# A two-layer attention network on one core: layer 1's weight product at the start, biases as rows, and the order of VectorE's work in the FFN

## The chip, the cores and the metric

The kernel runs on one core of one Trainium2 chip. The metric is the device time of one execution in microseconds (us), as a median over several runs. One further execution was profiled; durations quoted from the trace belong to that one.

## What is computed

The input is x, 8 images of 32x32 pixels with 384 channels, so 1024 tokens of 384 channels an image. The reference, cut to what matters:

```python
x = x + L0(_gn(x))                       # layer 0, _gn: group norm, 32 groups
t = tokens(x)
t = t + L1_attn(_ln_t(t), Wq, Wk, Wv)    # layer 1, _ln_t: layer norm
t = t + L1_ffn(_ln_t(t))

# L0: 6 heads of 64
q, k, v = split(x @ qkv_w + qkv_b)
attn = (q * SCALE) @ k.T + rel_h + rel_w # rel_h, rel_w: q times relative position tables
out = softmax(attn) @ v
return out @ proj_w + proj_b

# L1_attn: one head of 384, causal
q, k, v = x @ Wq, x @ Wk, x @ Wv
return softmax(causal(q @ k.T * 384**-0.5)) @ v

# L1_ffn
h = gelu(bitlinear(x, W1, b1))
return bitlinear(h, W2, b2)

# bitlinear: W by the sign of W - mean, per group; then the result is scaled
# by its absolute maximum (per group of images) and clipped
y = x @ sign(W - mean(W)).T + b
return clip(y * QB / (max(abs(y)) + EPS), -QB + EPS, QB - EPS)
```

The FFN works in five groups of 8 // 5 = 1 image, so images 0 to 4 go through it; the others receive zeros from it.

## The kernel before

**Tiles and stages.** Images are taken in the order 5, 0, 1, 2, 3, 4, 6, 7. An image lies as channels on the 128 partitions: 3 slabs (NC = 3) of 128 channels by 1024 tokens, f_gnT in the profile. PSUM has one pool, ps_o, of eight buffers of one bank each (128x512 float32); every product of TensorE (PE) goes into the next of them that is free, by `o_tile`.

**Order.** The program is written as one stream, and a scheduler places the instructions on the engines and gives each tile a buffer. `behind_of(i)` and `tc.issue_after(i)` bind an instruction to stand behind instruction i in the order. Each engine then runs its instructions in order and waits by semaphores. DMAs are issued by SyncE (SP) and ScalarE (ACT), each in its own order.

**Start.** `run` calls `load_T` (three slabs of image 5, 512 KB each), then `load_weights`: the biases bqk, bv and b1 on ACT's queue, read element by element into one column for each 128 channels; the two relative position tables `rel`; and on SP's queue the three thirds of qkv_w (wq_sb, raw_1, raw_2; 576 KB each), wproj, proj_b as pb, wv and b2. `group_norm_T` makes statistics on VectorE (DVE) (L401, L402), averages over a group with two small products on PE (gmean L405, gvar L413), and normalises the slabs (L418). GpSimd (POOL) makes combinations of the weights for the products below (`weight_forms`).

**Layer 0.** Queries: f_qk (L508), 24 passes for the first, then the relative tables f_rel. Keys and values are made by 15 products (A to F, f_pr_A to f_pr_F) of combined weights with combined inputs; ACT and DVE combine their results (parts n0 to n6, m5 and so on: f_u_n, f_u_m) into f_k and f_v (L752). When the last copy of the values is made, ACT runs a one-column exponential `early` (L783), so that the table of the exponential is there. It reads the part n5, which DVE makes (L589).

`attend0_fast` goes over three pairs of heads and two halves of the queries. For each, `scores(p, c, half)` makes eight column tiles c: two score tiles, one for each head of the pair, with two matmuls each (f_s, L830 and L834), then one exponential each on ACT (L841) into f_pr. `add_up` sums on DVE (L846, L848), `values` multiplies by f_v (f_av, L856), and `reciprocals` gives the denominators.

**Joint bias and joint weights.** For the first image alone, `join_biases` multiplies the values' bias by wproj and adds proj_b (matmuls L357, addition L360 on DVE); it stands after the products of image 5. `multiply_out` loads the transposed Wq and Wk of layer 1 on SP's queue and multiplies them once to wqk (L371, 18 passes; scaled on DVE, L372), which later gives layer 1 queries against its inputs without keys. It stands after the first eight calls of `scores` of image 5.

**FFN.** For a token tile j of 128 tokens, `activate` makes the gelu twice on ACT (L1170): `hi`, rounded to a shorter format, and the exact value; DVE takes the residue `lo` (L1171). The second product y2 (L1188) multiplies hi and lo; DVE adds the bias (L1189) and takes the absolute maximum of the tile (L1190, am2). Tile 0 is cut in three parts, later tiles in two. In the program tile j's activations stand before its matmuls, and its bias addition before tile j + 1's activations.

Of the kernel before, what the change touches and what calls it, by code (L numbers as in the profile page):

```python
# [11 lines left out]
F32 = mybir.dt.float32  # L12
# [79 lines left out]
def conv_attn_hybrid(  # L92
# [37 lines left out]
    wqkv_sb = wf.rearrange("p r s o -> p (r s o)")[:, : NC * 3 * C].rearrange("p (k o) -> p k o", k=NC)  # L130
    bqk, bqk_neg, bv, b1_sb = (tile_of(n, [P, w]) for n, w in (("bqk", 6), ("bqk_neg", 6), ("bv", NC), ("b1_sb", NM)))
    pb, b2_sb = tile_of("pb", [P, C]), tile_of("b2_sb", [P, C])
# [4 lines left out]
    def load_weights(pools):  # L137

        nc.scalar.dma_start(out=bqk, in_=qkv_b[0 : 2 * C].rearrange("(m p) -> p m", p=P))
        nc.vector.memset(rel, 0.0)  # L140
        for half in range(2):
            nc.scalar.dma_start(out=rel[half * HD : (half + 1) * HD, 0, : 2 * H - 1], in_=rel_hT)
            nc.scalar.dma_start(out=rel[half * HD : (half + 1) * HD, 1, : 2 * W - 1], in_=rel_wT)
        nc.scalar.dma_start(out=bv, in_=qkv_b[2 * C : 3 * C].rearrange("(m p) -> p m", p=P))
        nc.scalar.dma_start(out=b1_sb, in_=b1.rearrange("(m p) -> p m", p=P))
        src = qkv_w.rearrange("(p k) o -> p k o", k=NC)
        raw = [wq_sb]
        for i in range(3):
            if i:
                raw.append(pools.flat(f"raw_{i}")[:, : NC * C].rearrange("p (k o) -> p k o", k=NC))  # L150
            nc.sync.dma_start(out=raw[i], in_=src[:, :, ts(i, C)])
        nc.sync.dma_start(out=wproj_sb, in_=proj_w.rearrange("(k p) o -> p k o", p=P))
        nc.sync.dma_start(out=pb, in_=proj_b.partition_broadcast(P))
        nc.sync.dma_start(out=wv_sb, in_=wv.rearrange("(k p) o -> p k o", p=P))
        nc.sync.dma_start(out=b2_sb, in_=b2.partition_broadcast(P))

        nc.scalar.mul(bqk[:, 0:NPAIR], bqk[:, 0:NPAIR], qscale)
        nc.scalar.mul(bqk_neg, bqk, -1.0)
        nc.scalar.mul(rel, rel, 1.0 / qscale)
        early = pools.small.tile([P, 1], F32, tag="early", name="early_root")  # L160
        nc.scalar.activation(early, ones[:, 0:1], AF.Sqrt)
        return raw
# [199 lines left out]

    def multiply_out(pools):
        both = pools.flat("wqkT")
        wqT_sb, wkT_sb = (both[:, i * NC * C : (i + 1) * NC * C].rearrange("p (k c) -> p k c", k=NC) for i in range(2))
        nc.sync.dma_start(out=wqT_sb, in_=wqT.rearrange("(k p) c -> p k c", p=P))
        nc.sync.dma_start(out=wkT_sb, in_=wkT.rearrange("(k p) c -> p k c", p=P))
        for m in range(NC):
            ps = pools.o_tile(f"wqk_{m}")
            for k in range(NC):  # L370
                nc.tensor.matmul(ps[:, :C], wqT_sb[:, k, ts(m, P)], wkT_sb[:, k, :], start=(k == 0), stop=(k == NC - 1))  # L371
            nc.vector.tensor_scalar_mul(wqk[:, m, :], ps[:, :C], C**-0.5)  # L372

    def stages(pools):

        last_transpose = [None]

# [16 lines left out]
        def group_norm_T(b, xT=None):  # L394
# [17 lines left out]
            ps = pools.o_tile(f"gvar_{b}")  # L412
            nc.tensor.matmul(ps[:, 0:1], over_group, d[:, 1:2], start=True, stop=True)  # L413
            nc.vector.tensor_scalar_add(d[:, 0:1], ps[:, 0:1], 1e-5)
# [207 lines left out]
        def layer0(b, xT):  # L622
# [133 lines left out]
            def products():  # L756
# [25 lines left out]
                with behind_of(of_v.last_copy):  # L782
                    exp_loaded[0] = nc.scalar.activation(early, of_v.part["n5"][:, 0:1], AF.Exp, scale=0.0).ins  # L783

# [16 lines left out]
            for p in () if pools.fast else range(1, NPAIR):  # L801
                later(p, None, None)
            if pools.fast and b == ORDER[0]:
                join_biases(pools)

            def residual():
# [7 lines left out]
        def attend0_fast(residual, b, q, k, r, v, later):  # L814
# [72 lines left out]
            for p, half in itertools.product(range(NPAIR), range(2)):  # L887
                t, last = ts(half, 512), (p, half) == (NPAIR - 1, 1)
                prs = [scores(p, c, half) for c in range(NJ)]
                if b == ORDER[0] and (p, half) == (0, 0):  # L890
                    multiply_out(pools)
                if b == ORDER[0] and (p, half) == (2, 0):
# [223 lines left out]
        def ffn(xt, b, gn):  # L1116
# [45 lines left out]

            last_gelu = [None]

            def activate(room, j, m0, m1):
                part = pairs[j // 2][:, m0:m1, j % 2, :]
                hi, lo = (room[:, i, m0:m1, :] for i in range(2))
                for dst in (hi, part):
                    with behind_of(last_gelu[0]):
                        last_gelu[0] = nc.scalar.activation(dst, part, AF.Gelu, scale=s).ins  # L1170
                nc.vector.scalar_tensor_tensor(lo, part, QB - QEPS, hi.bitcast(F32), ALU.min, ALU.subtract)  # L1171
                return [[(h[:, m - m0, :], w2m[m]) for m in range(m0, m1)] for h in (hi, lo)]

            y = pools.flat(f"y2_{b}")[:, : NJ * C].rearrange("p (j c) -> p j c", j=NJ)
            am2 = pools.small.tile([P, NJ], F32, tag="am2", name=f"am2_{b}")
            for j in range(NJ):
                ps = pools.o_tile(f"y2_{b}_{j}")
                room = pools.flat(f"hilo_{b}_{j}", F32R)[:, : 3 * T].rearrange("p (i m q) -> p i m q", i=2, q=P)
                if j == 0:
                    (hi0, lo0), (hi1, lo1), (hi2, lo2) = (activate(room, j, *cut) for cut in ((0, 3), (3, 6), (6, NM)))  # L1180
                    products = hi0 + hi1 + lo0 + lo1 + hi2 + lo2
                else:
                    products = [t for cut in ((0, 6), (6, NM)) for kind in activate(room, j, *cut) for t in kind]
                if j == 4:
                    xt = pools.flat(f"xagain_{b}")[:, : NJ * C].rearrange("p (j c) -> p j c", j=NJ)
                    nc.sync.dma_start(out=xt.rearrange("p j c -> p (j c)"), in_=spilt)
                for i, (h, w) in enumerate(products):
                    nc.tensor.matmul(ps[:, :C], h, w, start=(i == 0), stop=(i == len(products) - 1))  # L1188
                nc.vector.tensor_tensor(y[:, j, :], ps[:, :C], b2_sb, ALU.add)  # L1189
                nc.vector.tensor_reduce(am2[:, j : j + 1], y[:, j, :], AX.X, ALU.max, apply_absolute_value=True)  # L1190
# [27 lines left out]

        def run(pools):
            gn = load_T(ORDER[0])  # L1220
            if pools.fast:
                raw = load_weights(pools)
                plain.append(raw[0])
            else:
                load_plain()
                plain.append(wqkv_sb)
            for _ in group_norm_T(ORDER[0], gn):
                pass
            if pools.fast:
                xf[ORDER[0]] = image_forms(ORDER[0], gn, nc.vector)  # L1230
                with tc.issue_after(weight_forms(pools, nc.gpsimd, raw[1], 1)):
                    weight_forms(pools, nc.gpsimd, raw[2], 2)
                make_unit(pools)
                make_fold()
# [86 lines left out]
```

## Time and profile before

| what | value |
|---|---|
| median of 3 runs | 2328.33 us (2328.3 to 2329.42) |
| profiled execution, its own time | 2329.14 us |
| its span in the trace | 2326.9 us |
| PE busy | 2296.9 us (99%) |
| DVE, ACT, POOL busy | 1530.0 (66%), 1098.6 (47%), 416.0 (18%) |
| granted clock of PE, mean | 0.998 |
| DMA | 185.82 MB in 156242 packets, of which 113568 under 512 bytes; mean 80 GB/s |

The profile page gives each engine's busy time and its share of the span. The view of waits sums for each line of an engine how long it stood idle and what ended the wait: total, times, longest. The chain follows the work that ended last from the last instruction back to what released it. The timeline lists groups of instructions by start; the numbers are the start, the time that the group takes (until its last instruction ends), the engine, the line, the operation and its tiles. Names such as f_qk are the tiles' names in the program with the image left out; PEld is PE's loading of weights, POOL is GpSimd.

### The profile page before, as it was taken

The page shows a single profiled execution, that of the slowest core. Times are in us where ns is not written, and L with a number is a line of the kernel's source. Part 1 is how long each engine was busy: PE and PEld are TensorE (multiplying, and loading weights), DVE is VectorE, ACT ScalarE, POOL GpSimd, SP SyncE. Part 2 cuts the span into 40 slices and gives each one's busy share as a digit, 9 for nine tenths or more (in the row PEclk, how much of TensorE's full clock was granted, in tenths as well). Part 3 has the DMA queues.
Part 4 walks back from the last instruction along what each step waited for, and adds up shares of the span by engine and source line. Part 5 has one row for each costly group of instructions (what it writes and reads, how often), then busy time and mean ns, then how long its engine had stood idle before and what let it go on. Part 6 is the DMA issues. An engine that isn't in the chain of part 4 may idle for free.

```text
span 2326.9 us, 27722 instructions
## 1 busy us (share of the span) xinstructions
PE 2296.9 (99%) x9970; PEld 1318.8 (57%) x9970; DVE 1530.0 (66%) x2434; ACT 1098.6 (47%) x1874; POOL 416.0 (18%) x520
## 2 busy tenths in 40 slices
PE   7999999999999999999999999999999999999998
PEld 3545554558645577545685455774457754555454
DVE  6785578575887347884458864588834788527851
ACT  4551166137563257642376522757324666116611
POOL 4320322030140201310102302013020131021300
PEclk9999999999999999999999999999999999999999
DMA  6530471140630114520308202064002262017100
GB/s 158 157 92 26 135 155 37 55 163 28 145 100 28 42 67 109 130 62 1 109 28 179 67 27 95 22 156 109 28 27 82 80 156 64 1 48 161 37 1 29
DMA packets 156242, 185.82 MB, mean 80 GB/s; under 512 B 113568, under 2 KB 126208, under 8 KB 153280
## 3 DMA queue, kind: packets, MB, share of 16 engines
q1 hardware_dynamic: 135856, 114.66, 20.0%
q0 software_dynamic: 17184, 69.22, 9.5%
q8 instruction: 82, 1.34, 0.2%
q14 instruction: 64, 0.52, 0.1%
q10 hardware_dynamic: 3056, 0.08, 0.1%
HBM read 83.24 MB, written 50.33 MB: 57 GB/s over the span
## 4 chain that ended last, share of the span: by engine, by line
PE 97%; DVE 1%; ACT 1%; DMA 0%; issue 0%; POOL 0%; ACTq 0%
PE f_s L830 14%; PE f_av L856 14%; PE f_s L1018 8%; PE f_av L1033 8%; PE f_y L1143 7%; PE f_y L1188 7%; PE f_pj L455 5%; PE f_v L455 5%; PE f_q L977 5%; PE f_qk L508 5%; PE f_s L834 4%; PE f_pr_A L508 4%; PE f_pr_B L508 3%; PE f_rel L508 2%; PE f_pt L383 1%; PE f_pr_D L508 1%
## 5 line engine op out<-in xcount | busy, mean ns | idle before, releaser
L841 ACT ACTIVATE f_pr<-f_s 128x512 f32<-128x512 f32 x768 | 412.7, 595 | 40.4 <-PE f_s L834 35.2
L830 PE MATMUL f_s<-f_q,f_k 64*128 64x512 f32 x1536 | 401.5, 595 | 0.4 <-DVE f_v L752 0.2
L848 DVE TENSOR_TENSOR f_sum<-f_sum,f_pr 128x1024 f32<-128x1024 f32 x288 | 365.0, 1267 | 22.9 <-ACT f_pr L841 0.7
L856 PE MATMUL f_av<-f_pr,f_v 128*64 128x512 f32 x1536 | 339.3, 594 | 0.0
L834 PE MATMUL f_s<-f_r,unit 64*128 64x512 f32 x768 | 310.3, 791 | 0.0
L830 PEld LDWEIGHTS f_s<-f_q,f_k 64*128 64x128 f32 x1536 | 148.0, 186 | 125.9 <-issue 64.0
L856 PEld LDWEIGHTS f_av<-f_pr,f_v 128*64 128x64 f32 x1536 | 106.2, 137 | 196.3 <-issue 192.4
L1018 PE MATMUL f_s<-f_q,f_lnT 128*128 128x512 f32 (+3 forms) x576 | 195.9, 488 | 0.0
L1033 PE MATMUL f_av<-f_v,f_pr 128*128 128x385 f32 x576 | 195.3, 486 | 0.0
L1027 ACT ACTIVATE f_pr<-f_s 128x512 f32<-128x512 f32 (+3 forms) x96 | 46.9, 491 | 279.0 <-DVE f_s L1023 233.4
L726 POOL DMA_DIRECT2D f_r<-f_far x192 | 102.3, 535 | 403.9 <-DVE f_far L720 190.7
L1033 PEld LDWEIGHTS f_av<-f_v,f_pr 128*128 128x128 f32 x576 | 108.3, 190 | 77.2 <-issue 11.5
L1018 PEld LDWEIGHTS f_s<-f_q,f_lnT 128*128 128x128 f32 x576 | 102.0, 190 | 77.8 <-issue 53.8
L1154 DVE TENSOR_REDUCE am<-f_h 128x1 f32<-128x1024 f32 (+2 forms) x80 | 71.6, 946 | 95.8 <-ACT f_h L1147 95.8
L1188 PE MATMUL f_y<-f_w2a,f_hilo 128*128 128x384 f32 x640 | 128.9, 342 | 5.5 <-DVE f_hilo L1171 5.3
L1147 ACT ACTIVATE f_h<-f_y,b_sb 128x256 f32<-128x256 f32 x240 | 100.8, 472 | 67.0 <-PE f_y L1143 67.0
L508 PE MATMUL f_qk<-f_gnT,wq_sb 128*128 128x512 f32 x288 | 129.4, 601 | 1.5 <-DVE f_gnT L418 1.5
L977 PE MATMUL f_q<-f_lnT,wqk 128*128 128x512 f32 x288 | 127.5, 592 | 0.0
L455 PE MATMUL f_pj<-wproj_sb,f_oT 128*128 128x384 f32 x384 | 127.3, 488 | 0.0
L834 PEld LDWEIGHTS f_s<-f_r,unit 64*128 64x128 f32 x768 | 76.5, 187 | 89.5 <-issue 89.3
L455 PE MATMUL f_v<-wv_sb,f_lnT 128*128 128x384 f32 x384 | 126.5, 486 | 0.0
L519 POOL TENSOR_TENSOR f_xf<-f_gnT 128x512 f32<-128x512 f32 x28 | 35.5, 1277 | 503.0 <-DVE f_gnT L418 503.0
(215 smaller groups left out, 3517.6 us busy)
## 6 DMA issues: line engine op xcount, KB each, us to landing
f_far<-f_far SPq DMA_DIRECT2D x48, 512.0 KB, 5.0
f_r<-f_far SPq DMA_DIRECT2D x192, 128.0 KB, 2.9
f_r<-f_far POOLq DMA_DIRECT2D x192, 128.0 KB, 4.6
f_gnT<-in_xT SPq DMA_DIRECT2D x24, 512.0 KB, 4.6
f_far<-f_far SPq DMA_DIRECT2D x192, 64.0 KB, 4.7
f_x<-in_x SPq DMA_DIRECT2D x32, 384.0 KB, 7.9
f_w1a<-w1s POOLq DMA_DIRECT2D x5, 1536.0 KB, 6.9
f_w2a<-w2s POOLq DMA_DIRECT2D x5, 1536.0 KB, 9.1
```

Source lines behind the costliest of these rows:

```text
L455: nc.tensor.matmul(ps[:, :C], xT[:, k, ts(j, P)], w[:, k, cols], start=(k == 0), stop=(k == NC - 1))
L508: last_product[0] = nc.tensor.matmul(*args, **kw).ins
L830: nc.tensor.matmul(sc[par], k[rows[par], p, ts(c, P)], q[rows[par], p, ts(half, 512)], start=True, stop=False)
L834: last_matmul[0] = nc.tensor.matmul(sc[par], unit[rows[par], c // 2 % 2].rearrange("i h w -> i (h w)"), r(2 * (c // 4) + c % 2, p)[rows[pa ...
L841: last_exp[0] = nc.scalar.activation(pr[:, ts(par, 512)], sc[par], AF.Exp).ins
L848: adds.append(nc.vector.tensor_tensor(total, total, pr, ALU.add).ins)
L856: last_matmul[0] = nc.tensor.matmul(av[ts(par, HD), :], v[:, c, ts(2 * p + par, HD)], pr[:, ts(par, 512)], start=(c == 0), stop=(c == NJ - 1),
L977: nc.tensor.matmul(ps, wqk[:, k, ts(m, P)], xT[:, half, k, :], start=(k == 0), stop=(k == NC - 1))
L1018: nc.tensor.matmul(sc[:, lo:], xT[:, c // 4, k, ts(c % 4, P)], q[:, half, k, lo:], start=(k == 0), stop=(k == NC - 1),)
L1033: nc.tensor.matmul(av[:, : C + 1], prs[c][:, ts(j - c, P)], v[:, c, :], start=(c == 0), stop=(c == j))
L1143: nc.tensor.matmul(ps, w1k[i // 2][:, ts(m, P)], xs[i % 2][:, half, i // 2, :], start=(i == 0), stop=(i == 2 * NC - 1))
L1188: nc.tensor.matmul(ps[:, :C], h, w, start=(i == 0), stop=(i == len(products) - 1))
```

## The change

- `load_factors`, split off from `multiply_out`, is called first in `run`, ahead of the first image: wqT on SP's queue, wkT on ACT's. `multiply_out` follows right after `load_weights`.
- The biases are loaded as 21 rows of 128 elements (9 of qkv_b, 12 of b1), transposed by PE into one bank and copied by DVE into `biases`, of which bqk, bv and b1_sb are columns.
- wproj is loaded ahead of qkv_w. `join_biases` is called after the first group norm, bound behind the product gvar of it (`last_mean`).
- `early` reads the part n6, which ACT makes, in place of n5.
- In the FFN, tile j + 1's activations stand in the program ahead of tile j's bias addition, and that addition is bound behind the first residue (`first_lo`) of tile j + 1.

```diff
--- before.py
+++ after.py
@@ -128,7 +128,8 @@
     wproj_sb, wv_sb = (tile_of(n, [P, NC, C]) for n in ("wproj_sb", "wv_sb"))
     wf, wq_sb = tile_of("wf", [P, N_PROD, 2, P]), tile_of("wq_sb", [P, NC, C])
     wqkv_sb = wf.rearrange("p r s o -> p (r s o)")[:, : NC * 3 * C].rearrange("p (k o) -> p k o", k=NC)
-    bqk, bqk_neg, bv, b1_sb = (tile_of(n, [P, w]) for n, w in (("bqk", 6), ("bqk_neg", 6), ("bv", NC), ("b1_sb", NM)))
+    biases, bqk_neg = tile_of("biases", [P, 3 * NC + NM]), tile_of("bqk_neg", [P, 6])
+    bqk, bv, b1_sb = biases[:, : 2 * NC], biases[:, 2 * NC : 3 * NC], biases[:, 3 * NC :]
     pb, b2_sb = tile_of("pb", [P, C]), tile_of("b2_sb", [P, C])
 
     rel = tile_of("rel", [P, 2, 2 * H])
@@ -136,24 +137,27 @@
 
     def load_weights(pools):
 
-        nc.scalar.dma_start(out=bqk, in_=qkv_b[0 : 2 * C].rearrange("(m p) -> p m", p=P))
         nc.vector.memset(rel, 0.0)
+        rows = pools.page("rows")[: 3 * NC + NM, :P]
+        nc.scalar.dma_start(out=rows[: 3 * NC, :], in_=qkv_b.rearrange("(m p) -> m p", p=P))
+        nc.scalar.dma_start(out=rows[3 * NC :, :], in_=b1.rearrange("(m p) -> m p", p=P))
         for half in range(2):
             nc.scalar.dma_start(out=rel[half * HD : (half + 1) * HD, 0, : 2 * H - 1], in_=rel_hT)
             nc.scalar.dma_start(out=rel[half * HD : (half + 1) * HD, 1, : 2 * W - 1], in_=rel_wT)
-        nc.scalar.dma_start(out=bv, in_=qkv_b[2 * C : 3 * C].rearrange("(m p) -> p m", p=P))
-        nc.scalar.dma_start(out=b1_sb, in_=b1.rearrange("(m p) -> p m", p=P))
+        nc.sync.dma_start(out=wproj_sb, in_=proj_w.rearrange("(k p) o -> p k o", p=P))
         src = qkv_w.rearrange("(p k) o -> p k o", k=NC)
         raw = [wq_sb]
         for i in range(3):
             if i:
                 raw.append(pools.flat(f"raw_{i}")[:, : NC * C].rearrange("p (k o) -> p k o", k=NC))
             nc.sync.dma_start(out=raw[i], in_=src[:, :, ts(i, C)])
-        nc.sync.dma_start(out=wproj_sb, in_=proj_w.rearrange("(k p) o -> p k o", p=P))
         nc.sync.dma_start(out=pb, in_=proj_b.partition_broadcast(P))
         nc.sync.dma_start(out=wv_sb, in_=wv.rearrange("(k p) o -> p k o", p=P))
         nc.sync.dma_start(out=b2_sb, in_=b2.partition_broadcast(P))
 
+        ps = pools.o_tile("biases")
+        nc.tensor.transpose(ps[:, : 3 * NC + NM], rows, ident[: 3 * NC + NM, : 3 * NC + NM])
+        nc.vector.tensor_copy(biases, ps[:, : 3 * NC + NM])
         nc.scalar.mul(bqk[:, 0:NPAIR], bqk[:, 0:NPAIR], qscale)
         nc.scalar.mul(bqk_neg, bqk, -1.0)
         nc.scalar.mul(rel, rel, 1.0 / qscale)
@@ -360,11 +364,14 @@
         nc.vector.tensor_tensor(pb, pb, ps[:, :C], ALU.add)
 
 
-    def multiply_out(pools):
+    def load_factors(pools):
         both = pools.flat("wqkT")
         wqT_sb, wkT_sb = (both[:, i * NC * C : (i + 1) * NC * C].rearrange("p (k c) -> p k c", k=NC) for i in range(2))
         nc.sync.dma_start(out=wqT_sb, in_=wqT.rearrange("(k p) c -> p k c", p=P))
-        nc.sync.dma_start(out=wkT_sb, in_=wkT.rearrange("(k p) c -> p k c", p=P))
+        nc.scalar.dma_start(out=wkT_sb, in_=wkT.rearrange("(k p) c -> p k c", p=P))
+        return wqT_sb, wkT_sb
+
+    def multiply_out(pools, wqT_sb, wkT_sb):
         for m in range(NC):
             ps = pools.o_tile(f"wqk_{m}")
             for k in range(NC):
@@ -373,7 +380,7 @@
 
     def stages(pools):
 
-        last_transpose = [None]
+        last_transpose, last_mean = [None], [None]
 
         def transpose_tiles(dst, srcs, engine):
 
@@ -410,7 +417,7 @@
             nc.vector.scalar_tensor_tensor(d[:, 1:2], d[:, 0:1], d[:, 0:1], mv[:, 1:2], ALU.mult, ALU.add)
             yield xT
             ps = pools.o_tile(f"gvar_{b}")
-            nc.tensor.matmul(ps[:, 0:1], over_group, d[:, 1:2], start=True, stop=True)
+            last_mean[0] = nc.tensor.matmul(ps[:, 0:1], over_group, d[:, 1:2], start=True, stop=True).ins
             nc.vector.tensor_scalar_add(d[:, 0:1], ps[:, 0:1], 1e-5)
             nc.scalar.activation(d[:, 0:1], d[:, 0:1], AF.Sqrt)
             nc.vector.reciprocal(cs[:, 1:2], d[:, 0:1])
@@ -780,7 +787,7 @@
                 of_v.run(N_PROD, put_values)
                 early = pools.small.tile([P, 1], F32, tag="early", name=f"early0_{b}")
                 with behind_of(of_v.last_copy):
-                    exp_loaded[0] = nc.scalar.activation(early, of_v.part["n5"][:, 0:1], AF.Exp, scale=0.0).ins
+                    exp_loaded[0] = nc.scalar.activation(early, of_v.part["n6"][:, 0:1], AF.Exp, scale=0.0).ins
 
             if pools.fast:
                 products()
@@ -800,9 +807,6 @@
 
             for p in () if pools.fast else range(1, NPAIR):
                 later(p, None, None)
-            if pools.fast and b == ORDER[0]:
-                join_biases(pools)
-
             def residual():
                 xt = load_x(pools, b)
                 for j in range(NJ):
@@ -887,8 +891,6 @@
             for p, half in itertools.product(range(NPAIR), range(2)):
                 t, last = ts(half, 512), (p, half) == (NPAIR - 1, 1)
                 prs = [scores(p, c, half) for c in range(NJ)]
-                if b == ORDER[0] and (p, half) == (0, 0):
-                    multiply_out(pools)
                 if b == ORDER[0] and (p, half) == (2, 0):
                     signs.append(binarize(pools))
                     next(signs[0])
@@ -1160,7 +1162,7 @@
 
 
 
-            last_gelu = [None]
+            last_gelu, first_lo = [None], [None]
 
             def activate(room, j, m0, m1):
                 part = pairs[j // 2][:, m0:m1, j % 2, :]
@@ -1168,25 +1170,33 @@
                 for dst in (hi, part):
                     with behind_of(last_gelu[0]):
                         last_gelu[0] = nc.scalar.activation(dst, part, AF.Gelu, scale=s).ins
-                nc.vector.scalar_tensor_tensor(lo, part, QB - QEPS, hi.bitcast(F32), ALU.min, ALU.subtract)
+                made = nc.vector.scalar_tensor_tensor(lo, part, QB - QEPS, hi.bitcast(F32), ALU.min, ALU.subtract)
+                if m0 == 0:
+                    first_lo[0] = made.ins
                 return [[(h[:, m - m0, :], w2m[m]) for m in range(m0, m1)] for h in (hi, lo)]
 
             y = pools.flat(f"y2_{b}")[:, : NJ * C].rearrange("p (j c) -> p j c", j=NJ)
             am2 = pools.small.tile([P, NJ], F32, tag="am2", name=f"am2_{b}")
-            for j in range(NJ):
-                ps = pools.o_tile(f"y2_{b}_{j}")
+
+            def activated(j):
                 room = pools.flat(f"hilo_{b}_{j}", F32R)[:, : 3 * T].rearrange("p (i m q) -> p i m q", i=2, q=P)
                 if j == 0:
                     (hi0, lo0), (hi1, lo1), (hi2, lo2) = (activate(room, j, *cut) for cut in ((0, 3), (3, 6), (6, NM)))
-                    products = hi0 + hi1 + lo0 + lo1 + hi2 + lo2
-                else:
-                    products = [t for cut in ((0, 6), (6, NM)) for kind in activate(room, j, *cut) for t in kind]
+                    return hi0 + hi1 + lo0 + lo1 + hi2 + lo2
+                return [t for cut in ((0, 6), (6, NM)) for kind in activate(room, j, *cut) for t in kind]
+
+            products = activated(0)
+            for j in range(NJ):
+                ps = pools.o_tile(f"y2_{b}_{j}")
                 if j == 4:
                     xt = pools.flat(f"xagain_{b}")[:, : NJ * C].rearrange("p (j c) -> p j c", j=NJ)
                     nc.sync.dma_start(out=xt.rearrange("p j c -> p (j c)"), in_=spilt)
                 for i, (h, w) in enumerate(products):
                     nc.tensor.matmul(ps[:, :C], h, w, start=(i == 0), stop=(i == len(products) - 1))
-                nc.vector.tensor_tensor(y[:, j, :], ps[:, :C], b2_sb, ALU.add)
+                if j + 1 < NJ:
+                    products = activated(j + 1)
+                with behind_of(first_lo[0]):
+                    nc.vector.tensor_tensor(y[:, j, :], ps[:, :C], b2_sb, ALU.add)
                 nc.vector.tensor_reduce(am2[:, j : j + 1], y[:, j, :], AX.X, ALU.max, apply_absolute_value=True)
             s, ga = absmax_scale(am2, f"2_{b}")
 
@@ -1217,9 +1227,11 @@
         plain = []
 
         def run(pools):
+            factors = load_factors(pools) if pools.fast else None
             gn = load_T(ORDER[0])
             if pools.fast:
                 raw = load_weights(pools)
+                multiply_out(pools, *factors)
                 plain.append(raw[0])
             else:
                 load_plain()
@@ -1227,6 +1239,8 @@
             for _ in group_norm_T(ORDER[0], gn):
                 pass
             if pools.fast:
+                with tc.issue_after(last_mean[0]):
+                    join_biases(pools)
                 xf[ORDER[0]] = image_forms(ORDER[0], gn, nc.vector)
                 with tc.issue_after(weight_forms(pools, nc.gpsimd, raw[1], 1)):
                     weight_forms(pools, nc.gpsimd, raw[2], 2)
```

## The prediction

> **What bounds the kernel now.** I read the page's shares and its chain first, because they say which engine sets the end:
>
> ```profile
> PE 2296.9 (99%) x9970; PEld 1318.8 (57%) x9970; DVE 1530.0 (66%) x2434; ACT 1098.6 (47%) x1874; POOL 416.0 (18%) x520
> ...
> PE 97%; DVE 1%; ACT 1%; DMA 0%; issue 0%; POOL 0%; ACTq 0%
> ```
>
> TensorE (PE) works 2296.9 of 2326.9 us, and 97% of the chain that ended last is PE. So the change can gain only by removing PE work or a PE wait, and every new PE wait costs its full length. The view of waits, for PE alone, lists what there is to remove:
>
> ```profile
> PE f_gmean L405 <- DVE gmv L402: 11.5, 1, 11.5
> PE f_y L1188 <- DVE f_hilo L1171: 5.3, 5, 1.1
> ```
>
> The first is the idle start, the second one wait of 1.1 us in each of the five FFNs. Third, the chain of the first 32 us:
>
> ```profile
> 0.81 4.25 DMA f_gnT<-in_xT
> ...
> 5.07 4.50 DMA f_gnT<-in_xT
> ...
> 11.53 0.57 PE f_gmean L405 x2
> ...
> 12.78 0.60 PE f_gvar L413 x2
> ...
> 14.90 12.00 PE f_qk L508 x24
> 26.90 1.92 PE f_rel L508 x8
> ```
>
> PE stands idle until the image's slabs have landed and the statistics are made. Then it runs 24 f_qk passes in 12.00 us. The same 24 take 10.46 us at 268.47, in a busy stretch: 1.54 us of the 12.00 belong to the cold start. Fourth, the timeline of image 0 around the first scores, and DVE's longest wait there:
>
> ```profile
> 65.38 2.10 PE L357 MATMUL f_pb<-wproj_sb,bv 128*128 128x384 f32 x6
> ...
> 78.70 6.07 PE L371 MATMUL f_wqk<-f_wqkT 128*128 128x384 f32 x18
> 84.71 1.51 PE L856 MATMUL f_av<-f_pr,f_v 128*64 128x512 f32 x6
> ```
> ```profile
> DVE pb L360 <- PE f_pb L357: 8.2, 1, 8.2
> ```
>
> The joint bias is six passes between the last product and the first scores (65.38 to 67.41, 2.03 us). Its addition blocks DVE for 8.2 us, with v's combinations (L752) queued behind it. The scores then need those: 67.41 to 78.70 is 11.29 us, against 8.94 in image 1 (317.44 to 326.38).
>
> **Image 0 loses work: -10.4 us.** Moved out are pb's 2.03 and the 18 wqk passes from 78.70 to 84.71, 6.01. DVE no longer stands behind the pb matmul, so the excess of the first scores goes, 11.29 - 8.94 = 2.35. Sum 10.39. All of it is on PE with PE work on both sides, so it counts in full. The two factor loads also leave SP's queue in image 0; nobody there waits for what stood behind them.
>
> **The start takes it up: +2.1 us.** The factors are 1.18 MB, put ahead of the image's slabs. From 2 to 18 us the DMA share is about 1 and 290 GB/s move on average, so 1.18 MB push everything by 4.1 us. In return the biases come as rows: the 4-byte elements were some 2700 packets, and their queue used 2.3% of all 16 engines over 80 us, 1.84 us. Net +2.2: statistics end at 11.4 + 2.2 = 13.6 instead of 11.4. wproj and wq move back as far, to about 16, still ahead of their readers. On SP the third slab now stands behind the landing of the bias rows, which is no later than its old predecessor's; raw_1 and raw_2, and with them POOL's weight forms (from 15.27), move by about the 2 us that their readers move too. On ACT the rows and wkT are issued ahead of rel and of ACT's first table load; rel is read at 26.83 and ACT's sqrt stands at 13.60, so both have room.
>
> The factors land at about 7.0 (2 us plus 4.1, and a share lost to the first slab beside them). The biases' one transpose waits for rows of 4.5 us landing and is over by then. The 18 wqk passes are 6.01 us warm; cold I add the 1.54 that f_qk paid, so they end at 7.0 + 7.6 = 14.6 (rounded). gmean stands behind them on PE, and its statistics (13.6) are there, so gmean starts at 14.6 and not 11.5. DVE has the three wqk scalings (1.48 together) in front of the gcs copy; the last needs the last wqk matmul and lies beside gmean's 0.57. From gmean to f_qk 3.37 us pass as before. The pb matmuls (2.03) now lie between gvar and f_qk, where PE was idle 1.52: 0.51 more. f_qk starts at 18.5, 3.6 late; the array has been busy, so it takes 10.46 and f_rel is 2.1 late. Bounds: +0.6 if the factors land at 5.5, +5 if they land at 8.5 and f_qk is cold again. The pb addition and the bias copy on DVE are under 0.6 us each (0.56 for the 128x384 addition L1189) and lie beside f_qk or the loads.
>
> Two rules bear on this start. The chain's f_qk rows show what cold costs, 1.54 us once. The Trainium skill ("TensorE: Matmul & The Clock Gate", Part 1) says the array runs at half clock until it has been busy through a window of about 3.4 us, and falls back after an idle one; by that figure wqk would lose an estimated 1.7 us instead of 1.54, and f_qk as much again should the gap before it fill a window, which is a rule against the move.
> The DMA rows show a share of 1 already. The skill's first page ("Trainium Kernel Development and Optimization", Key Constraints) says that SP's and ACT's queues share the same 16 engines, so that wkT on ACT's queue saves issue time only; were it otherwise, the start would gain up to half of 4.1 us.
>
> **FFN: -5.3 us.** The timeline of the first FFN's second token tile shows the wait:
>
> ```profile
> 561.58 0.56 DVE L1189 TENSOR_TENSOR f_y<-f_y,b_sb 128x384 f32<-128x384 f32 x1 [1.40 <-PE f_y L1188]
> 562.17 0.55 DVE L1190 TENSOR_REDUCE am<-f_y 128x1 f32<-128x384 f32 x1
> 562.64 1.82 DVE L1171 SCALAR_TENSOR_TENSOR f_hilo<-f_h,f_hilo 128x768 fp32r<-128x768 f32 x2
> ...
> 563.64 1.66 PE L1188 MATMUL f_y<-f_w2a,f_hilo 128*128 128x384 f32 x8 [1.06 <-DVE f_hilo L1171]
> ```
>
> The residue of tile 1 had its inputs at 560.99 and stood behind the bias addition of tile 0, which waits for PE. Put ahead of it, it ends at 561.96, before PE asks for it at about 562.5. Five FFNs lose 1.06 each. Queued behind the residue are now the addition and the reduction of tile j; ps_o has eight banks and y2 uses one a tile, so nobody waits. ACT needs 3.72 us a tile against PE's 4.0 to 4.2 and stays the cover; without it 0.
>
> **The edit with the large price: +1.95 us in each of eight images.** `early` (L783) now reads n6, which ACT itself made, in place of n5, which DVE makes. In the program as built this also changes which PSUM banks the first scores of every image receive. Before, column tile c=1 took two banks that v's products had left long ago. Now c=1 takes the banks of c=0 and waits for its two exponentials, and the first half of c=2 waits for the first exponential of c=1; c=3 on finds banks free. Image 1's rows give the price:
>
> ```profile
> 317.44 1.13 PE L830 MATMUL f_s<-f_q,f_k 64*128 64x512 f32 x4
> ...
> 318.64 1.02 PE L830 MATMUL f_s<-f_q,f_k 64*128 64x512 f32 x4
> 318.89 2.11 ACT L841 ACTIVATE f_pr<-f_s 128x512 f32<-128x512 f32 x4 [1.68 <-PE f_s L834]
> ...
> 319.72 1.04 PE L830 MATMUL f_s<-f_q,f_k 64*128 64x512 f32 x4
> ```
>
> c=0's first exponential runs from 318.89 to 319.49 (0.595), so c=1 starts at 319.6 instead of 318.64. Its scores end 1.36 later at 320.96, its first exponential at 321.65, and c=2 starts at about 321.7 instead of 319.72: 1.98 late. From there ACT (0.527 an exponential, 1.05 a tile) keeps ahead of PE (1.09 a tile), so the delay neither grows nor shrinks, and the values that follow begin as much later. Nothing PE-bound behind it gives it back. I take 1.95; the bounds are 0.95 (c=2's wait hidden) and 2.4 (a further 0.2 of signalling at each of two waits). Nothing in the trace of before shows this wait, so 0 can't be excluded either.
>
> **Sum:** -10.4 + 2.1 - 5.3 + 8 x 1.95 = +2.0 us. Against the profiled execution's 2329.14 that is 2331.1; the median lies 0.81 lower, so 2330.3. This kernel's measurement tells about 0.2%, 4.7 us, from no change.
>
> **Rivals.** *Faster:* the bank wait costs one step of 0.95 or nothing, because the banks' releases come earlier than I read. Then the sum is -10.4 + 2.1 - 5.3 + 7.6 = -6.0 (2322.3), or -13.6 (2314.7) at nothing. For it: no such wait stands in the old trace, and at (0,1) banks are reused with no loss. Against: there the exponentials run a tile behind, here PE and ACT must alternate. I give 0.18.
> *Slower:* the alternation at the first scores costs 2.4 in each of eight images, with the start at +5: -10.4 + 5 - 5.3 + 19.2 = +8.5 (2336.8). It decides once the wait exceeds 2.3 us an image (+4.8 with my other terms). For it: every step has a semaphore on either side. Against: exponentials start 0.09 us behind their scores here. I give 0.24.
> *Not what it says:* the FFN wait stays, since ACT is the true pace: +2.0 + 5.3 = +7.3 (2335.6). ACT's 3.72 a tile speaks against it; 0.06.
>
> **How the numbers follow.** My case has 0.52; its bounds (start 0.6 to 5, wait 1.5 to 2.3) give -3 to +7.5, of which I put 0.35 within 0.2%, 0.14 above and 0.03 below. The faster rival gives 0.17 below and 0.01 within; the two slower ones 0.27 above and 0.03 within. Together 0.20 faster, 0.39 same, 0.41 slower. The range 2320.5 to 2337.5 leaves out the nearly free bank wait below and the sum of both slower rivals above. My case alone: 2325.3 to 2335.8.
>
> **What would show it.** Right: PE's waits list f_s L830 behind ACT f_pr with 16 entries or more and some 15 us; no f_y behind f_hilo; av(0,0) of image 0 about 6.3 us earlier; f_rel near 29. Wrong: no PE wait on ACT at the first scores (then 2315 to 2322), or f_rel past 32.

## The result and the profile after

The changed kernel takes 2334.31 us (median of 11 runs, 2331.99 to 2337.59) against 2328.88 (11 runs, 2328.15 to 2330.12): a ratio of 1.0022, 95% interval 1.0013 to 1.0032. That is 5.4 us slower, at the edge of what the prediction called no change. The profiled execution took 2332.19 us, span 2330.3, and is one of the fastest of the eleven. Images are counted here as in the prediction, from 0 in the order in which the kernel takes them: image 0 is the input's image 5. Line numbers moved by a few: the scores' L830 and L834 are L834 and L838 now, their exponentials' L841 is L845.

The view of waits of the changed kernel, PE alone (engine and line, what it waited for: us in total, times, longest):

```profile
PE f_s L834 <- ACT f_pr L845: 9.4, 16, 0.7
PE f_biases L159 <- DMA f_rows<-in_b: 7.6, 1, 7.6
...
PE f_gvar L420 <- DVE gd L417: 1.0, 1, 1.0
```

The wait for the statistics (11.5) and that for the residues (5.3) are gone; at the start PE now waits 7.6 for the bias rows. The first line is the new wait that the prediction named: 16 waits of the scores for the exponentials, two in each of eight images. The timeline of image 1's first scores shows both (last column: idle time before, and what ended it):

```profile
313.66 1.18 PE L834 MATMUL f_s<-f_q,f_k 64*128 64x512 f32 x3 [0.67 <-ACT f_pr L845]
...
315.99 1.13 PE L834 MATMUL f_s<-f_q,f_k 64*128 64x512 f32 x4 [0.49 <-ACT f_pr L845]
...
317.19 1.02 PE L834 MATMUL f_s<-f_q,f_k 64*128 64x512 f32 x4
```

c=1 starts at 313.66, c=2 at 315.99, 2.33 later, and c=3 only 1.20 after that; before the change c=1 and c=2 stood 1.08 apart. After c=2 the pace is the old one. The list's 9.4 us count PE's idle time alone. The loss is larger, because the passes behind a wait overlap less: c=1's six passes took 1.85 us here (313.66 to 315.51) and 1.27 before (318.64 to 319.91). ACT's rows show the other half of the alternation, two exponentials at a time with an idle stretch ahead of each pair:

```profile
313.01 1.09 ACT L845 ACTIVATE f_pr<-f_s 128x512 f32<-128x512 f32 x2 [2.36 <-PE f_s L838]
315.34 1.08 ACT L845 ACTIVATE f_pr<-f_s 128x512 f32<-128x512 f32 x2 [1.25 <-PE f_s L834]
```

The start, from PE's timeline (cold, below, means before the granted clock's step to 1; in the kernel before, the first f_qk passes start 0.85 us apart, and 0.43 apart behind that step at 17.82):

```profile
7.81 7.50 PE L378 MATMUL f_wqk<-f_wqkT 128*128 128x384 f32 x18
15.14 0.28 PE L412 MATMUL f_gmean<-gmv,over_group 128*128 128x1 f32 x2
16.47 0.38 PE L420 MATMUL f_gvar<-gd,over_group 128*128 128x1 f32 x2 [1.05 <-DVE gd L417]
16.71 2.18 PE L361 MATMUL f_pb<-wproj_sb,biases 128*128 128x384 f32 x6
18.73 10.46 PE L515 MATMUL f_qk<-f_gnT,wq_sb 128*128 128x512 f32 x24
29.12 1.99 PE L515 MATMUL f_rel<-f_q,rel 64*128 64x512 f32 x8
```

And DVE in the first FFN: the second tile's residue at 557.28 stands ahead of the first tile's bias addition, and waits only for ACT.

```profile
557.28 0.96 DVE L1173 SCALAR_TENSOR_TENSOR f_hilo<-f_h,f_hilo 128x768 fp32r<-128x768 f32 x1 [0.84 <-ACT f_h L1172]
558.15 0.55 DVE L1199 TENSOR_TENSOR f_y<-f_y,b_sb 128x384 f32<-128x384 f32 x1
```

Laid side by side, the two traces give each stretch its shift. The table is worked out from the starts of the same PE groups in both (f_rel 26.83 and 29.12; the first scores 67.41 and 67.77; the first values 84.71 and 78.87; an FFN from the first pass of y2 to the next image's f_rel; and so on):

| stretch | predicted, us | measured, us |
|---|---|---|
| start, to the first f_rel | +2.1 | +2.29 |
| image 0, from there to its first values | -10.4 + 1.95 = -8.45 | -1.94 - 6.19 = -8.13 |
| first scores of images 1 to 7 | 7 x 1.95 = +13.65 | 7 x 2.19 = +15.3 |
| five FFNs | -5.3 | -1.33 -1.48 -1.43 -1.40 -1.43 = -7.1 |
| small shifts elsewhere (the rest) | 0 | +1.0 |
| span | +2.0 | +3.4 |

The profiled run accounts for 3.4 of the 5.4 us. The rest, and the spread of 5.6 us where before had 2, is in runs that this trace doesn't show.

### The profile page after: what moved, and what is told of

Read it like the earlier page. It is cut to its first block, busy times and chain, and to the rows that moved or that the text cites. A ratio compares the mean times of both kernels' runs of the same rounds, so it can differ in the third digit from the quotient of the medians.

```text
span 2330.3 us, 27731 instructions
## 1 busy us (share of the span) xinstructions
PE 2301.2 (99%) x9971; PEld 1318.5 (57%) x9971; DVE 1530.3 (66%) x2435; ACT 1099.7 (47%) x1874; POOL 426.7 (18%) x520
## 4 chain that ended last, share of the span: by engine, by line
PE 97%; ACT 1%; DVE 1%; DMA 0%; issue 0%; ACTq 0%; POOL 0%; DVEq 0%
PE f_s L834 15%; PE f_av L860 14%; PE f_s L1020 8%; PE f_av L1035 8%; PE f_y L1145 7%; PE f_y L1195 7%; PE f_pj L462 5%; PE f_v L462 5%; PE f_q L979 5%; PE f_qk L515 5%; PE f_s L838 4%; PE f_pr_A L515 4%; PE f_pr_B L515 3%; PE f_rel L515 2%; PE f_pt L390 1%; PE f_pr_D L515 1%
## 5 line engine op out<-in xcount | busy, mean ns | idle before, releaser
L845 ACT ACTIVATE f_pr<-f_s 128x512 f32<-128x512 f32 x768 | 413.7, 595 | 59.7 <-PE f_s L838 45.9
L834 PE MATMUL f_s<-f_q,f_k 64*128 64x512 f32 x1536 | 404.4, 597 | 9.4 <-ACT f_pr L845 9.4
L838 PE MATMUL f_s<-f_r,unit 64*128 64x512 f32 x768 | 310.2, 791 | 0.0
L834 PEld LDWEIGHTS f_s<-f_q,f_k 64*128 64x128 f32 x1536 | 146.6, 186 | 140.8 <-issue 64.7
L1035 PEld LDWEIGHTS f_av<-f_v,f_pr 128*128 128x128 f32 x576 | 108.2, 190 | 77.3 <-issue 11.5
L1149 ACT ACTIVATE f_h<-f_y,biases 128x256 f32<-128x256 f32 x240 | 100.9, 472 | 67.4 <-PE f_y L1145 67.4
L850 DVE TENSOR_TENSOR f_sum<-f_pr,f_pr 128x1024 f32<-128x1024 f32 x48 | 62.1, 1293 | 102.8 <-ACT f_pr L845 102.8
L838 PEld LDWEIGHTS f_s<-f_r,unit 64*128 64x128 f32 x768 | 76.3, 187 | 89.4 <-issue 89.4
```

What stands on the lines that cost most here:

```text
L834: nc.tensor.matmul(sc[par], k[rows[par], p, ts(c, P)], q[rows[par], p, ts(half, 512)], start=True, stop=False)
L838: last_matmul[0] = nc.tensor.matmul(sc[par], unit[rows[par], c // 2 % 2].rearrange("i h w -> i (h w)"), r(2 * (c // 4) + c % 2, p)[rows[pa ...
L845: last_exp[0] = nc.scalar.activation(pr[:, ts(par, 512)], sc[par], AF.Exp).ins
L1035: nc.tensor.matmul(av[:, : C + 1], prs[c][:, ts(j - c, P)], v[:, c, :], start=(c == 0), stop=(c == j))
```

## The experiments

All times below are medians beside runs of the kernel before on the same chip (2329.2 to 2329.5). My theory was the bank wait as the loss, with the start and the FFN as the gains; the rival was that the loss lay in the start or in the order of the FFN.

**n5 again.**

```diff
-exp_loaded[0] = nc.scalar.activation(early, of_v.part["n6"][:, 0:1], AF.Exp, scale=0.0).ins
+exp_loaded[0] = nc.scalar.activation(early, of_v.part["n5"][:, 0:1], AF.Exp, scale=0.0).ins
```

> The changed kernel with one edit taken back: `early` reads n5 again. In the program as built, the first scores of every image get the banks of v's products again, as before the change. Bank theory: the 2.2 us that images 1 to 7 each lost at their first scores go, and 2.2 in image 0: 8 x 2.2 = 17 us less than the changed kernel, so about 2317 us, 12 under the kernel before, and no PE wait on f_pr at the first scores. Rival (the loss lies in the start and the FFN's order, the banks cost nothing): time stays at 2332 to 2334. On the spread of the changed kernel's runs (2332 to 2337.6): if the bank wait makes it, it shrinks to that of before (some 2 us); if the start makes it, it stays some 5 us.

Measured: 2316.52 us (2315.73 to 2317.8), ratio 0.9946 (0.9933 to 0.996). Against the changed kernel that is 17.8 less; the traces show 2.17 to 2.22 less from the first scores to the first values of each of the eight images. No wait of f_s is left in PE's list:

```profile
PE f_biases L159 <- DMA f_rows<-in_b: 7.5, 1, 7.5
PE f_bad L271 <- DVE worst L269: 1.9, 1, 1.9
PE f_gvar L420 <- DVE gd L417: 1.3, 1, 1.3
```

One character decides the sign: without it the change gains 12.7 us. The spread of the five runs is 2 us.

**n6 alone**, the same edit made to the kernel before.

> The kernel before with only the read of n5 turned into n6. The program as built gives c=1 the banks of c=0 in all images. Bank theory: 7 x 2.2 = 15.3 us more, and in image 0 between 0 and 2.2 more (the scores wait there on v's combinations anyway): 2344 to 2346 us, with 14 to 16 waits of f_s on f_pr. Rival (the exponential table being ready earlier is a gain or nothing): 2328 to 2329. If the bank wait makes the runs' spread, it shows here as 5 us.

Measured: 2346.55 us (2345.13 to 2349.65), ratio 1.0075 (1.0061 to 1.0089). From the first scores to the first values, six of the images 1 to 7 lose 2.18 to 2.21, image 5 loses 3.85. The spread of 4.5 us came with the edit. Its trace shows a source, in the view by windows around image 0's first scores (window; its length; then busy time of PE, PEld, DVE, ACT, POOL; PEclk, the granted clock; DMA):

```profile
68.95:72.36 3.41, 2.43 (x10) 1.14 (x10) 3.34 (x7) 2.02 (x4) 0.00 (x0) 1.00 0.46 70
72.36:75.77 3.41, 3.41 (x12) 1.99 (x10) 1.95 (x3) 1.23 (x3) 0.00 (x0) 0.50 0.70 182
75.77:79.18 3.41, 3.41 (x22) 2.38 (x20) 2.65 (x3) 2.94 (x6) 0.00 (x0) 1.00 0.09 32
```

PE was busy for 2.43 of 3.41 us while it alternated with ACT; for the next 3.41 us the granted clock was 0.5, and they hold 12 passes of PE where the 3.41 us after them hold 22. The same happened from 1584.46 to 1587.88, in image 5. The mean granted clock of each of the five runs fits: it falls from 0.999 (2345.13 and 2345.52 us) over 0.998 and 0.997 to 0.996 (2349.65) as the time rises.

**The changed kernel once more.**

> The changed kernel once more, for a second trace. Its eleven runs spread over 2332 to 2337.6, and the trace of the kernel before with n6 alone holds two stretches of 3.41 us at a granted clock of 0.5 within first scores, where that image lost 3.8 us instead of 2.2. Clock theory: each such stretch costs some 1.65 us, and a run at 2332 has none, one at 2337 three: this trace shows (time - 2332) / 1.65 of them, all in first scores. Rival (the wait itself varies in length): no such stretch, and per-image losses that differ from 2.2.

Measured: 2335.77 us, span 2333.9: 3.57 more than in the first trace. 1.7 of them came between the first scores and the first values of image 6, in one stretch of 3.41 us at 0.5:

```profile
1884.47:1887.89 3.42, 2.24 (x10) 1.10 (x10) 0.23 (x1) 1.99 (x4) 0.00 (x0) 1.00 0.70 100
1887.89:1891.30 3.41, 3.41 (x12) 1.43 (x10) 1.38 (x2) 1.27 (x3) 0.00 (x0) 0.50 0.12 13
```

The expectation asked for two of them, (2335.77 - 2332) / 1.65. The other 2.0 us lie at the start: the record of the granted clock has its first entry, the step to 1, at 13.97 us there and at 10.72 in the first trace, so that wqk took 9.10 us instead of 7.50 and f_rel came at 31.10, not 29.12. Where the stretches of 3.41 us lie may decide this: PE was busy for 3.11 of the 3.41 us up to 10.72 in the first trace, but for 2.92 of the 3.42 up to 10.56 in this one, and the clock rose a stretch later; in the kernel before, 2.92 of 3.41 up to 17.82 sufficed.

So there are two sources. The falls in first scores come with the bank wait: none of the eleven traces of kernels with n5 has a fall between 25 us and its last 9 us, and the three with n6 have none, one and two. The other source comes with any cold start. What decides which image is hit stayed open. Busy time by the modelled ends does not: in this same trace PE was busy for 2.24 us from 942.40 to 945.81 as well, in the first trace for 2.25 us from 68.75 to 72.16, and the clock fell behind neither.

**The FFN alone**, `activated`, `first_lo` and the order of the bias addition put into the kernel before.

> The kernel before with only the FFN's part of the change. From the two traces the five FFNs are 1.3 to 1.5 us shorter each, 6.9 together: 2322 us, and no wait of f_y on f_hilo. By the prediction's own term it would be 5.3: 2323.6. Rival (the FFN's gain came from elsewhere in the change): 2329.

Measured: 2323.37 us (2322.58 to 2324.27), ratio 0.9974 (0.9965 to 0.9984). That is 5.8 less, nearer to the prediction's 5.3 than to 6.9. The trace, the longest of the ten runs, shows 1.20 to 1.41 less at each of the five FFNs, 6.6 together. Its f_qk took 13.51 us at the start, not 12.00, which hides 1.5 of that in this trace; the starts of the other runs were not traced.

**The start alone**: the changed kernel with the FFN and n5 of before.

> The kernel before with only the start's part: factors first, wqk there, biases as rows, the joint bias after the group norm; the FFN's order and n5 as before. From the two traces: start +2.3, pb -2.0, wqk -6.0, the rest of image 0's first scores -2.35: 8 us less, 2320.5. If the start makes the spread of the changed kernel's runs, it shows here as 5 us.

Measured: 2322.97 us (2321.61 to 2323.71), ratio 0.9973 (0.9962 to 0.9984), 2.5 above the expected. 1.6 of that are in its trace: the bias rows came 0.5 later than in the changed kernel (8.11 for 7.61), wqk ran cold for longer (8.37 us for 7.50), and f_rel was 3.86 late, not 2.29. Image 0's own part came out at -1.94 - 8.38 = -10.3, against -10.4 predicted. FFN and start together, -5.8 and -6.2, make the -12.7 of the kernel with n5 but for 0.7.

**Biases element by element**, in the kernel with n5.

```diff
-nc.scalar.dma_start(out=rows[: 3 * NC, :], in_=qkv_b.rearrange("(m p) -> m p", p=P))
+nc.scalar.dma_start(out=biases[:, : 3 * NC], in_=qkv_b.rearrange("(m p) -> p m", p=P))
...
-nc.tensor.transpose(ps[:, : 3 * NC + NM], rows, ident[: 3 * NC + NM, : 3 * NC + NM])
...
```

> The changed kernel with n5 (2316.5 us) and the biases loaded element by element again, without the transpose. The prediction's term (the 4-byte packets take 1.84 us of all DMA engines): the statistics end 1.8 us later, about 14.8 instead of 13.0, which wqk on PE (to 15 to 16.5) hides; wqk itself starts when the factors land, not the rows: together -1 to +0.5, 2315.5 to 2317. Rival (the packets were on the path): 2318.5.

Measured: 2317.95 us (2317.53 to 2318.69), 1.4 more than with rows, at the rival's side. The elements landed 8.7 us after issue, the rows 5.3. SP's third slab waits for that landing (chain of this run: slab issued at 10.07, when the first elements had landed), so its statistics began at 13.95, not 11.15, and PE did wait for them, 0.9 us. Two short idle gaps followed each other, and the clock was at 0.5 from 18.45 to 21.87: pb took 3.45 us instead of 2.18. The elements cost through their share of the DMA engines, which were fully busy from 8.5 to 9.5 us with no more than 18 GB/s, through the queue, since from 9.5 to 11 their share was under 0.2 while the third slab was awaited, and through the clock.

**The joint bias at its old place**, in the kernel with n5.

> The changed kernel with n5 (2316.5 us) and the joint bias at its old place behind the products. By the prediction's terms: 2.03 back between products and scores and 2.35 back at the first scores for DVE's backlog, less 0.5 to 0.7 at the start: +3.8, 2320.3. Rival (the backlog at the first scores came from wqk or something else): +1.4, 2318.

Measured: 2322.92 us (2322.12 to 2324.25), 6.4 more, where 3.8 were expected. Between products and scores +1.94 and at the first scores +2.38 returned, as the prediction had them (2.03 and 2.35). Most of the difference is f_qk, 13.51 us against 10.46; this run's wqk, 7.47 against 8.98, took half of that back. With pb gone from the gap behind gvar, PE stood idle there, and

```profile
18.70 13.51 PE L515 MATMUL f_qk<-f_gnT,wq_sb 128*128 128x512 f32 x24 [1.53 <-DVE f_gnT L425]
```

took 13.51 us; by the view of windows

```profile
11.00:17.82 6.82, 5.11 (x19) 3.09 (x17) 4.02 (x12) 3.49 (x7) 1.08 (x3) 1.00 1.04 366
17.82:24.64 6.82, 5.94 (x7) 2.52 (x8) 6.78 (x9) 0.42 (x1) 6.82 (x9) 0.50 0.24 88
```

the granted clock was 0.5 from 17.82 to 24.64.

**That gap filled with idle matmuls**, to tell the clock from another cause.

```diff
+some, ps = pools.page("fill"), pools.o_tile("fill")
+nc.gpsimd.memset(some, 0.0)
+with tc.issue_after(last_mean[0]):
+    for i in range(4):
+        nc.tensor.matmul(ps, some[:, :P], some[:, :512], start=(i == 0), stop=(i == 3))
```

> The kernel with the joint bias at its old place (2322.9 us, where the clock fell to 0.5 from 17.8 to 24.6 us and 24 f_qk passes took 13.5 instead of 10.3), with four idle matmuls (zeros, never read) between gvar and f_qk, where pb lies in the changed kernel. Clock theory: the gap before f_qk is filled, the clock stays at 1 and f_qk takes 10.3 again: 3 us less and at most 0.5 for the four, 2320.3, which was the sum without the clock. Rival (the slow f_qk had another cause): 2323.

Measured: 2322.88 us (2321.29 to 2323.37), no change in time. The mechanism shows all the same:

```profile
18.73 3.68 PE L1249 MATMUL f_fill<-f_fill 128*128 128x512 f32 x8
22.24 10.46 PE L515 MATMUL f_qk<-f_gnT,wq_sb 128*128 128x512 f32 x24
```

f_qk is back at 10.46. But I had mis-sized the four: a matmul of 128x512 is two passes of PE, eight in all, 3.68 us, and this run's wqk ran 1.4 us longer cold. What the clock gave, the filler took. That the filler kept the clock up rests on this one trace beside the one above.

**The transpose behind wqk**, in the kernel with n5 (`finish_biases` called after `multiply_out`).

> The changed kernel with n5 (2316.5 us) and the bias transpose behind wqk on PE, so that the rows' landing (7.5) no longer stands ahead of wqk. If the factors have landed by 6.5, wqk, gmean and f_rel come 1.2 us earlier: 2315.3. Rival (the factors land no earlier than the rows, or the clock starts as late anyway): 2316.5.

Measured: 2315.42 us (2314.39 to 2315.79), as expected: wqk started at 6.69 instead of 7.70.

**Six idle matmuls ahead of that**, from a tile of zeros.

> The changed kernel with n5 and the bias transpose behind wqk (2315.4 us), with six idle matmuls (zeros, never read, 0.85 us each cold) from about 1.2 to 6.3 us, while PE waits for the factors. Clock theory: the array is at full clock when wqk starts, wqk takes 6.0 to 6.5 instead of 8.6, gmean then waits for the statistics at about 13.0 instead of 15.4, and f_rel comes 2 to 2.4 us earlier: 2313.2, with less spread. Rival (the passes, not the clock, need 8.6, or the statistics are late anyway): 2315.4; if the clock falls again while gmean waits, 2316 to 2317.

Measured: 2314.91 us (2314.27 to 2316.03). wqk took 5.97 us instead of 8.57, as the clock theory has it. But the six were again twelve passes, 8.27 us, and held wqk until 9.63, so f_rel came at 29.61, no earlier than without them (29.17).

**wkT on SP's queue**, in the kernel with n5.

```diff
-nc.scalar.dma_start(out=wkT_sb, in_=wkT.rearrange("(k p) c -> p k c", p=P))
+nc.sync.dma_start(out=wkT_sb, in_=wkT.rearrange("(k p) c -> p k c", p=P))
```

> The changed kernel with n5 (2316.5 us) and wkT on SP's queue behind wqT. Theory of the prediction (16 engines shared, the queue saves issue time only): both factors land within 0.5 us of before, the slabs are issued about 0.6 later; 2316 to 2317.5. Rival (a second queue moves more): wkT lands 2 us or more later, wqk and f_rel with it, 2318.5.

Measured: 2314.48 us (2313.88 to 2315.18), ratio 0.9936 (0.9922 to 0.995): the shortest of all, 1.5 us under the expectation's lower end. The factors were hardly slower on one queue: wkT landed 5.5 us after its issue at 1.31 us, where on ACT's queue it had taken 5.6 from 0.82, and wqk started at 6.90. The rows, which now stand first on ACT's queue, were there for the transpose at 5.49 instead of 7.50. wqk also ran less cold, 7.92 us against 8.98. I take that for the start's chance and not the queue's doing, since the two traces of the changed kernel differ by more (7.50 and 9.10).

**Three idle matmuls ahead of that one.**

> The changed kernel with n5 and wkT on SP's queue (2314.5 us), with three idle matmuls ahead of the biases' transpose. A matmul of 128x512 was two passes of PE in the run with six, so three are six passes of 0.85 cold, from 1.5 to 6.6 us, just before the factors land (6.9). Clock theory: wqk takes 6.0 instead of 7.9, gmean waits for the statistics at 13.9 instead of 14.66, and f_rel comes 0.8 earlier: 2313.7. Rival: the clock rises no earlier, or falls while gmean waits: 2314.5 to 2316.

Measured: 2315.57 us (2313.38 to 2316.83): the rival. In the trace, which is of the longest of the five runs, wqk took 6.04, as expected, but then

```profile
14.71 0.39 PE L418 MATMUL f_gmean<-gmv,over_group 128*128 128x1 f32 x2 [1.96 <-DVE gmv L415]
...
16.26 4.19 PE L361 MATMUL f_pb<-wproj_sb,biases 128*128 128x384 f32 x6
20.24 11.21 PE L521 MATMUL f_qk<-f_gnT,wq_sb 128*128 128x512 f32 x24
```

PE waited 1.96 us for the statistics and 0.70 for the next step, the clock fell from 14.89 to 21.72, and pb took 4.19 us where it had taken 2.18. There a wqk that finished early only opened a gap. The four kernels between 2314.5 and 2315.6 lie within 1.1 us with overlapping ranges; what beats both kernels beyond doubt is the change with n5, 12.7 us under the kernel before, and 15 with wkT on SP's queue.

## Why the prediction was right, point by point

- **The bank wait** carried the verdict and was there in the place, number and size given: 16 waits, 2.19 us an image against 1.95. The steps inside were off by as little: c=1 came 0.84 late for 0.96, c=2 2.09 for 1.98. One sign to look for was mis-sized: the list shows 9.4 us, not some 15, because it holds idle time alone. That the edit of `early` causes it is shown in both directions, +17.4 on the kernel before and -17.8 on the changed one. That it acts through the banks is read from the programs as built, where c=1 has c=0's banks in just the kernels that read n6 (in image 0 of the changed kernel c=0, 1 and 2 get banks 4 and 3, 4 and 3, 4 and 0; with n5 4 and 3, 0 and 7, 5 and 2), and from the wait list, which names the exponentials that empty them. Why the planner hands out other banks when `early` reads n6 was not tested.
- **Image 0** was right term by term: -1.94 for pb, and -8.38 for wqk and DVE's backlog where the bank wait is away (2.03, and 6.01 + 2.35).
- **The start** was right in sum (+2.29 for +2.1), and its sketch held: wqk cold, 7.50 us; gmean behind it at 15.14 for 14.6; f_qk at 18.73 for 18.5 and warm. The statistics ended at 13.0, ahead of the 13.6 worked out. But the factors' landing was not what gated wqk. The bias rows were, at 7.61; my step that called the transpose "over by then" was wrong, and moving it gained 1.1 us.
- **The FFN's term was mis-sized**: -1.33 to -1.48 an FFN in the traces, not -1.06. I priced the idle time of PE alone; the trace's PEld entry beside it already showed 1.38 us of idle weight loading:

```profile
563.64 1.34 PEld L1188 LDWEIGHTS f_y<-f_w2a,f_hilo 128*128 128x128 f32 x8 [1.38 <-DVE f_hilo L1171]
```

The passes after the stall ran without their weights loaded ahead: the loads and the passes begin together at 563.64.
- **The clock was missing from the terms behind the start.** The likeliest case of 2330.3 was 4 us under the median. Terms that ran over by themselves (bank wait +1.65, small shifts +1.0, start and image 0 +0.5, less 1.8 in the FFN) make 1.4 of it; the changed kernel's median lies 2.1 above its profiled run; the last 0.5 is the median of before, 2328.88 with more runs. That the trace comes within 1.4 us of the sum is partly luck: what the FFN gave more than I had counted hid what the bank wait took more. For the 2.1 I had no term: falls of the clock in first scores at 1.7 each, and a start that runs cold for up to 2.0 us longer. Which of them the untraced runs had isn't shown; their mean granted clock fits, 0.997 in the three longest of the eleven (2335.72 to 2337.59) and 0.999 in two of the three shortest (2332.19 and 2332.22).
- **The rivals.** The free bank wait is refuted. The slower rival's point, 2.3 us an image, was not reached by the wait alone (2.19); with a fall of the clock an image reaches 3.9, and the medians' difference, +5.4, lies above the +4.8 at which I let that rival begin. A range of 17 us left room for either. "Not what it says" is refuted: no f_y wait on f_hilo is left.

On the rule named in the prediction: the Trainium skill ("TensorE: Matmul & The Clock Gate", Part 1) has the clock fall after an idle window of about 3.4 us. Here falls last 3.41 or 6.83 us, one or two such windows, which agrees, but those in first scores came after windows in which PE was busy for 2.24 and 2.43 us. By that window I had estimated 1.7 us for wqk's cold loss; it was 1.5 in the first trace and 3.1 in the second (7.50 and 9.10 us against 5.97 when warmed ahead). The same page's section "A second HAM failure mode: psum-queue depth-cycling" tells of a kernel that cycles through PSUM banks and whose short idles between groups of matmuls are enough for the clock to go down and up; the first scores look like such a case, though a rare one: three falls in 24 images.

The rule on queues (the Trainium skill, "Trainium Kernel Development and Optimization", Key Constraints: all queues run on the same 16 DMA engines) fits the run: wkT on SP's queue landed 0.4 us later, not the 2 or more of the rival.

## What to carry to other kernels

A dummy instruction that reads another tile can change which PSUM banks its successors get; compare the waits of the program as built around every reuse, in each repetition, since here 2.2 us in each of eight images outweighed the 12.7 us that the rest of the change gained. Where two engines hand the same two buffers to and fro, price the full alternation for each repetition. Where work is moved to a cold start, count which gap it fills as well as which it opens: a short wait costs its length, and now and then a stretch at half clock behind it.

## What the runs showed of the hardware

- The granted clock fell for stretches of 3.41 or 6.83 us after windows that were only partly idle: one with PE busy for 2.24 of 3.42 us was followed by a fall, another with 2.24 of 3.41 in the same trace was not. One such stretch in first scores cost 1.7 us (image 6 of the second trace, image 5 of n6 alone).
- At the start the clock reached 1 between 2.9 us (before: f_qk from 14.90, clock at 17.82) and 6.1 us (second trace of the changed kernel: wqk from 7.84, clock at 13.97) after PE's first real work; f_rel of the changed kernel moved by 2.0 us between its two traces.
- 21 rows of 128 elements landed 5.3 to 5.9 us after the issue of their second part with wkT ahead of them on the queue, and 4.0 us after it without (issue at 1.47, transpose at 5.49); the same 2688 elements one by one 8.7 us after it.
